# A graph network with feed-forward layers on one core: the norms, transposes and products of the two edge passes placed further apart, and the depth FFN on a line of its own

## The chip, the core and the metric

The program runs on one core of a Trainium2 chip. Five engines work side by side, each on its own queue in order: TensorE for matrix products (PE; its weight loads are listed as PEld), VectorE (DVE), ScalarE (ACT), GpSimd (POOL) and SyncE (SP, which here only issues DMAs). The measure is the device time of one execution in microseconds; a median of three runs stands for a kernel.

## The reference, cut to what matters

There are 12500 nodes of 256 numbers and 212500 edges, sorted by destination. Four layers follow each other, each on the layer norm of what came before, each added to it:

```python
edge_index = jnp.stack([src, dst])
x = x + _L0_gnn_ref(_layernorm(x), L0_gnn_weight, src, dst, edge_type_8, edge_weight)
x = x + _L0_ffn_ref(_layernorm(x)[None], ..., L0_ffn_wr, L0_ffn_br, L0_ffn_w1, L0_ffn_b1, L0_ffn_w2, L0_ffn_b2)[0]
x = x + _L1_gnn_ref(_layernorm(x), edge_index, L1_gnn_W, L1_gnn_att_src, L1_gnn_att_dst, L1_gnn_bias)
x = x + _L1_ffn_ref(_layernorm(x)[None], L1_ffn_Wg, L1_ffn_bg, L1_ffn_W1, L1_ffn_b1, L1_ffn_W2, L1_ffn_b2)[0]
```

- L0 gnn: for every edge the source row, multiplied by one of eight block-diagonal matrices and by the edge's weight, is summed at the destination.
- L0 ffn ("depths"): a score per node picks half of the nodes; for those `gelu(n @ w1 + b1) @ w2 + b2` with 1024 hidden units is weighted and added.
- L1 gnn: graph attention with 4 heads: softmax over the edges of a destination, weighted sum of the source rows, elu.
- L1 ffn: a gate of 8 experts; each node goes to its two best experts, 512 hidden units each.

## The kernel before, in words

**Stages.** First a table T0 of all eight products of every node is written to memory (97 stores of 1 MB). Then comes the first edge pass (`even_depths`), which also runs the depth FFN for every node; then the choice of the half (`choose`) and the combination; then the attention pass (`even_gat`), which also routes nodes to experts; last the experts (`slots`), 67 groups of 256 places.

**An edge pass.** Edges are taken in tiles of 128, 1661 of them. For each tile POOL gathers 128 rows from a table (L234), and PE multiplies them by a matrix S of 128 edges by 96 nodes (96 columns, each edge has a 1 or its weight at its destination; made by DVE for six tiles at once at L1012 and L1107). The products add up in PSUM in a bin of nodes (L1003): 512 nodes in the first pass, 256 in the second. A tile's window of 96 nodes sometimes lies across two bins; then each half has two products instead of one. In the trace every fp32 product of the program is two MATMUL and two LDWEIGHTS rows, so a tile has four rows, or eight across a bin's edge.

**Order.** The order on PE, DVE, ACT and SP is written out by hand. `Plan` is a list of (step, work); one step is one edge tile. At step t the gather of tile t is issued, at step t + 3 (first pass) its products follow. Gathers on POOL run free of this order: they wait only for a free buffer, of which the first pass has 16, one tile each; in the second pass a tile is fetched some 50 steps before it is used. A piece of work written as a generator goes on the plan too: `yield n` means that the rest comes n steps later. `Plan.queue(line, step, work)` runs the works of one line after each other. So when an engine's next instruction in this order has to wait, all that stands behind it on that engine waits too.

**When a bin of the first pass is full** (every 68 tiles), `summed` (L1046 to L1099) is queued on `line`: the node rows are loaded (SP), the sums copied out of PSUM (ACT L1052, DVE L1053), transposed back by PE (L195, `pt<-ident,aT`) and added to x (DVE L1060); the norm's statistics follow (DVE L214, L215, L201 to L208), then for each of up to four blocks of 128 nodes the normalized row `xn` (DVE L219), its transpose one step later (PE L195, `pt<-ident,xn`), the score (DVE L1073), x plus its norm (DVE L1075), and the copy into `xT` two steps later (L189 on ACT and L191 on DVE by turns). Then the FFN: for f of 8, two products with 512 columns (L1083) and the gelu (ACT L1085), one f every two steps; and for each block eight products with 256 columns (L1091) into a `pt` buffer, four to a step, then the bias (DVE L1097) and the store of Y (SP). The PSUM pools are `bin` (two buffers of two banks), `ph` (two) and `pt` (two).

**When 512 nodes of the attention pass are full**, `route` (L723 to L798) is queued on a line there. It computes the norm's statistics, and for each block `xn` (L219), one step later its transpose, one step later the copy to `xT`, one step later two products with 8 columns (L749) for the gate; then the choice on DVE, a count (L777, L778) and the scatter of the rows to their places (POOL).

Of the kernel before, what the change touches and what calls it, by code (L numbers as in the profile page):

```python
# [23 lines left out]
F32 = mybir.dt.float32  # L24
# [3 lines left out]
OP = mybir.AluOpType  # L28
# [7 lines left out]
P = 128  # L36
# [64 lines left out]
def gnn_ffn_kernel(ctx: ExitStack, tc: tile.TileContext, x, src, dst, etype, eweight, w_rel, wr, br,  # L101
                   fw1, fb1, fw2, fb2, W, att_src, att_dst, bias, Wg, bg, W1, b1, W2, b2, out):
    nc = tc.nc
    N, D = x.shape
# [88 lines left out]
    def transpose(o, i):  # L193
        k = i.shape[0]
        nc.tensor.transpose(o, i, ident[:k, :k])  # L195
# [22 lines left out]
    def normalized(o, xr, mv):  # L218
        nc.vector.tensor_scalar(o, xr, mv[:, 0:1], mv[:, 1:2], op0=OP.subtract, op1=OP.mult)  # L219
# [99 lines left out]
    with ExitStack() as pre:  # L319
# [63 lines left out]
        for i, (t, nat, around, dt) in enumerate(((NS, KSN, 0.0, F32), (NBR, NBN, -FAR, F32), (DM, DMN, 0.0, BF16))):  # L383
# [15 lines left out]
                                op=OP.subtract)  # L399
# [275 lines left out]
    def router(st):  # L675
# [50 lines left out]
        def route(ms, xg, wk, pst, psc, behind=None):  # L726


            G = len(ms)
            mv = wk.tile([P, 4, 2], F32, name="mv")  # L730
            ln_stats(xg[:, :, :D], mv[:, :G], wk)
            yield 3
            nc.vector.tensor_copy(xg[:, :G, D], node[:, ms[0]:ms[0] + G])
            nc.vector.tensor_copy(xg[:, :G, D + 1:], mv[:, :G, :])
            gt = wk.tile([P, 4, NE], F32, name="gt")
            pg = psc[0].tile([P, 4, NE], F32, name=psc[1])
            for i, m in enumerate(ms):
                xn = wk.tile([P, D], F32, name="xn")
                normalized(xn, xg[:, i, :D], mv[:, i, :])
                yield 1  # L740
                pt = pst[0].tile([P, 2, P], F32, name=pst[1])
                for k in range(2):
                    transpose(pt[:, k, :], xn[:, k * P:(k + 1) * P])
                yield 1
                xT = wk.tile([P, 2, P], F32, name="xT")
                evac(xT, pt)
                yield 1
                for k in range(2):
                    nc.tensor.matmul(pg[:, i, :], xT[:, k, :], Wgs[:, k, :], start=k == 0, stop=k == 1)  # L749
            yield 2  # L750
            nc.vector.tensor_tensor(gt[:, :G, :], pg[:, :G, :], bgB[:, None, :].to_broadcast([P, G, NE]), op=OP.add)

            mk = wk.tile([P, 4, NE], F32, name="mk")
            q1 = wk.tile([P, 4, NE, NE], F32, name="q1")
            q2 = wk.tile([P, 4, NE, NE], F32, name="q2")
            for i in range(G):
                mine = gt[:, i, :, None].to_broadcast([P, NE, NE])
                other = gt[:, i, None, :].to_broadcast([P, NE, NE])
                nc.vector.tensor_tensor(q1[:, i], other, mine, op=OP.is_equal)
                nc.vector.tensor_tensor(q2[:, i], other, mine, op=OP.is_gt)  # L760
            yield 1
            nc.vector.tensor_tensor(q1[:, :G], q1[:, :G], lower[:, :G], op=OP.mult)
            nc.vector.tensor_tensor(q2[:, :G], q2[:, :G], q1[:, :G], op=OP.add)
            nc.vector.tensor_reduce(mk[:, :G, :], q2[:, :G], axis=AX.X, op=OP.add)
            nc.vector.tensor_scalar(mk[:, :G, :], mk[:, :G, :], 1.5, None, op0=OP.is_lt)
            if rows(ms[-1]) < P:
                nc.vector.tensor_scalar(mk[:, G - 1, :], mk[:, G - 1, :], real, None, op0=OP.mult)
            yield 1
            pair = q1
            for i in range(G):  # L770
                nc.vector.tensor_tensor(pair[:, i], mk[:, i, :, None].to_broadcast([P, NE, NE]),
                                        mk[:, i, None, :].to_broadcast([P, NE, NE]), op=OP.mult)
            nc.vector.tensor_tensor(pair[:, :G], pair[:, :G], lower[:, :G], op=OP.mult)
            yield 1

            pp_ = psc[0].tile([P, 2, 4, NE, NE], F32, name=psc[1])
            nc.tensor.matmul(pp_[:, 0, :G], before, pair[:, :G], start=True, stop=True)  # L777
            nc.tensor.matmul(pp_[:, 1, :G], ones, pair[:, :G], start=True, stop=True)  # L778
            yield 2
            pos = q2  # L780
            for i in range(G):
                nc.vector.tensor_tensor(pos[:, i], pp_[:, 0, i], run, op=OP.add)
                nc.vector.tensor_tensor(run, pp_[:, 1, i], run, op=OP.add)
            yield 1
            nc.vector.tensor_tensor(pos[:, :G], pos[:, :G], turn[:, None].to_broadcast([P, G, NE, NE]), op=OP.mult)
            nc.vector.tensor_tensor(pos[:, :G], pos[:, :G], start[:, None].to_broadcast([P, G, NE, NE]), op=OP.add)
            nc.vector.tensor_tensor(pos[:, :G], pos[:, :G], pair[:, :G], op=OP.mult)
            to = wk.tile([P, 4], F32, name="to")
            nc.vector.tensor_reduce(to[:, :G], pos[:, :G].rearrange("p g e f -> p g (e f)"), axis=AX.X, op=OP.add)
            toI = wk.tile([P, 4], I32, name="toI")  # L790
            nc.vector.tensor_copy(toI[:, :G], to[:, :G])
            yield 3
            for i, m in enumerate(ms):
                n = rows(m)
                if i:
                    yield 2
                with tc.issue_after(behind().ins) if behind else nullcontext():
                    filled.append(to_slots(toI[:n, i:i + 1], xg[:n, i, :]))  # L798
# [227 lines left out]
    def even_depths(AD, lcC):  # L1026


        with ExitStack() as md:
# [8 lines left out]
            with ExitStack() as r1:  # L1038
# [2 lines left out]
                psA = r1.enter_context(tc.tile_pool(name="r1_pa", bufs=2, space=PSUM))  # L1041
                psh = r1.enter_context(tc.tile_pool(name="r1_ph", bufs=2, space=PSUM))
                pst = r1.enter_context(tc.tile_pool(name="r1_pt", bufs=2, space=PSUM))
                plan, line = Plan(), []

                def summed(b, sums):  # L1046
                    ms = [m for m in range(b * BIN // P, (b + 1) * BIN // P) if m < NM]
                    G = len(ms)
                    xg = wk.tile([P, 4, D], F32, name="xg")
# [1 line left out]
                    aT = wk.tile([P, 2, BIN], F32, name="aT")  # L1051
                    nc.scalar.activation(aT[:, 0, :G * P], sums[0][:, :G * P], AF.Copy)  # L1052
                    nc.vector.tensor_copy(aT[:, 1, :G * P], sums[1][:, :G * P])  # L1053
                    yield 3
                    for i, m in enumerate(ms):
                        pt = pst.tile([P, 2, P], F32, name="pt")
                        for k in range(2):
# [2 lines left out]
                        nc.vector.tensor_tensor(X[:, m, :], xg[:, i, :], pt.rearrange("p k j -> p (k j)"), op=OP.add)  # L1060
                    mv = wk.tile([P, 4, 2], F32, name="mv")
                    ln_stats(X[:, ms[0]:ms[0] + G, :], mv[:, :G], wk)
                    yield 1
                    xT = wk.tile([P, 2, 4 * P], F32, name="xT")
                    for i, m in enumerate(ms):
                        xn = wk.tile([P, D], F32, name="xn", bufs=2)
                        normalized(xn, X[:, m, :], mv[:, i, :])
                        yield 1
                        pt = pst.tile([P, 2, P], F32, name="pt")
                        for k in range(2):  # L1070
                            transpose(pt[:, k, :], xn[:, k * P:(k + 1) * P])
                        junk = wk.tile([P, D], F32, name="junk")
                        nc.vector.scalar_tensor_tensor(junk, xn, 1.0, wrB, op0=OP.mult, op1=OP.mult,  # L1073
                                                       accum_out=WT[:, m:m + 1])
                        nc.vector.tensor_tensor(X[:, m, :], X[:, m, :], xn, op=OP.add)  # L1075
                        yield 2
                        evac(xT[:, :, i * P:(i + 1) * P], pt)
                    yield 2
                    hT = wk.tile([P, KH, 4 * P], F32, name="hT")
                    for f in range(KH):  # L1080
                        ph = psh.tile([P, 4 * P], F32, name="ph")
                        for k in range(2):
                            nc.tensor.matmul(ph[:, :G * P], w1s[:, k, f * P:(f + 1) * P], xT[:, k, :G * P],  # L1083
                                             start=k == 0, stop=k == 1)
                        nc.scalar.activation(hT[:, f, :G * P], ph[:, :G * P], AF.Gelu_apprx_tanh, bias=b1s[:, f:f + 1])  # L1085
                        yield 2
                    yield 1
                    for i, m in enumerate(ms):
                        py = pst.tile([P, D], F32, name="pt")
                        for f in range(KH):  # L1090
                            nc.tensor.matmul(py, hT[:, f, i * P:(i + 1) * P], w2s[:, f, :],  # L1091
                                             start=f == 0, stop=f == KH - 1)
                            if f % 4 == 3:
                                yield 1
                        yield 1
                        y = wk.tile([P, D], F32, name="y", bufs=2)
                        nc.vector.tensor_tensor(y, py, b2B, op=OP.add)  # L1097
                        n = rows(m)
                        nc.sync.dma_start(Y[m * P:m * P + n, :], y[:n])  # L1099

# [705 lines left out]
```

## Time and profile before

| | us |
|---|---|
| median of 3 runs | 6287.21 (6270.61 to 6287.57) |
| the profiled execution's own time | 7111.5 |
| its span, first to last instruction | 7109.7 |
| first pass: first to last gather | 468.1 to 2909.2 |
| attention pass: first to last gather | 3178.8 to 5987.5 |
| last stage (experts): first to last product | 6128.6 to 7092.9 |
| mean granted TensorE clock | 0.733 |

The profiled execution is 824 us longer than the median, so a stage read from it is not a stage of the timed runs; what is worked out from it has to be carried over. The profile has, for each engine, the time in which it was busy; in its second part the span in 40 slices, with the clock that TensorE was granted in each; the chain of waits that ended last; and groups of instructions by line, with the mean of one. The trace behind it also gives these for any stretch of time, and the clock as a list of stretches at full and at half rate, each a whole number of 3.413 us long.

### The profile page before, as it was taken

How to read it: one execution, taken by the hardware profiler on the slowest of the kernel's cores; microseconds unless marked ns; L12 is line 12 of the kernel's file. 1: busy time of each engine (PE TensorE's matmuls, PEld its weight loads, DVE VectorE, ACT ScalarE, POOL GpSimd, SP SyncE). 2: the span in 40 equal slices, each digit the busy share in tenths (PEclk: the TensorE clock that was granted, in tenths of full speed). 3: DMA queues.
4: the chain of work that ended last, by engine and by line, in shares of the span. 5: the costliest groups of instructions: out<-in, count | busy, mean ns of one | idle time of the engine just before them, and what ended most of it. 6: DMA issues, size and time to landing. Idle time of an engine off the chain costs nothing.

```text
span 7109.7 us, 79724 instructions
## 1 busy us (share of the span) xinstructions
PE 5659.9 (80%) x28484; PEld 4914.0 (69%) x28484; DVE 3019.7 (42%) x7766; ACT 771.3 (11%) x1619; POOL 3699.1 (52%) x3731
## 2 busy tenths in 40 slices
PE   6977887787788877663777777878777778699999
PEld 3446666666677666553776777777777777688887
DVE  6642323223322333373555555556555555422221
ACT  2320000000000000040000000000000000122222
POOL 0026666666666666276656565666666564221111
PEclk9986877888778877785555555555565555799999
DMA  7763333333333333264444444444444443465553
GB/s 245 301 232 96 98 100 101 102 101 97 100 101 102 100 98 101 69 206 114 114 111 115 107 113 113 111 114 117 110 116 112 109 112 86 144 220 183 184 172 117
DMA packets 471792, 914.69 MB, mean 129 GB/s; under 512 B 83656, under 2 KB 307655, under 8 KB 458747
## 3 DMA queue, kind: packets, MB, share of 16 engines
q0 software_dynamic: 173280, 472.25, 23.9%
q1 hardware_dynamic: 298096, 437.15, 19.7%
q8 instruction: 230, 3.77, 0.2%
q14 instruction: 186, 1.52, 0.1%
HBM read 728.21 MB, written 185.63 MB: 129 GB/s over the span
## 4 chain that ended last, share of the span: by engine, by line
PE 55%; issue 17%; DVE 12%; another core or an unknown queue 9%; POOL 3%; DMA 2%; ACT 1%; SPq 0%; DVEq 0%; POOLq 0%; ACTq 0%
PE bin L1003 32%; PE pm L469 5%; PE ph L1083 5%; PE pt L1091 5%; PE pt L195 2%; DVE rows L1380 2%; POOL out_dram L946 1%; PE pt L749 1%; PE ph L932 1%; PE py L942 1%; DVE ln_st L214 1%; DVE S L1012 1%; PE px L1342 1%; PE py L1182 1%
## 5 line engine op out<-in xcount | busy, mean ns | idle before, releaser
L234 POOL DMA_INDIRECT rows<-T1A,srcC x1661 | 1644.0, 990 | 1053.1 <-issue 439.5
L234 POOL DMA_INDIRECT row<-T,rowC x1661 | 1649.4, 993 | 854.0 <-issue 306.0
L1003 PE MATMUL bin<-S,rows 128*128 128x96 f32 (+5 forms) x8756 | 1889.7, 388 | 244.8 <-issue 218.0
L1003 PEld LDWEIGHTS bin<-S,rows 128*128 128x128 f32 x8756 | 1814.5, 307 | 282.6 <-issue 252.9
L1003 PEld LDWEIGHTS bin<-S,row 128*128 128x128 f32 x7700 | 1247.4, 244 | 240.5 <-issue 219.5
L1003 PE MATMUL bin<-S,row 128*128 128x96 f32 (+5 forms) x7700 | 1263.2, 324 | 102.8 <-issue 99.6
L1012 DVE TENSOR_TENSOR S<-lcC,col 128x576 f32<-128x576 f32 x554 | 416.2, 751 | 501.6 <-PE bin L1003 212.2
L1380 DVE TENSOR_TENSOR rows<-rows,pw 128x1536 f32<-128x1536 f32 x277 | 483.2, 1745 | 120.0 <-remote 36.5
L195 PE MATMUL pt<-ident,xn 128*128 128x128 f32 x1052 | 225.7, 331 | 375.1 <-DVE xn L219 216.0
L1083 PE MATMUL ph<-xT,w1s 128*128 128x512 f32 (+1 forms) x800 | 419.0, 653 | 123.6 <-ACT hT L1085 79.1
L946 POOL DMA_INDIRECT out_dram<-y,toI x134 | 132.4, 988 | 698.2 <-DVE y L945 688.5
L932 PE MATMUL ph<-xT,we 128*128 128x256 f32 x2144 | 477.8, 381 | 2.0 <-DVE xT L191 2.0
L942 PE MATMUL py<-w,hT 128*128 128x256 f32 x2144 | 473.5, 379 | 0.0
L195 PEld LDWEIGHTS pt<-ident,xn 128*128 128x128 f32 x1052 | 155.9, 179 | 430.4 <-issue 290.2
L942 PEld LDWEIGHTS py<-w,hT 128*128 128x128 f32 x2144 | 407.4, 190 | 55.4
L932 PEld LDWEIGHTS ph<-xT,we 128*128 128x128 f32 x2144 | 405.0, 191 | 55.7 <-DVE xT L191 2.6
L1091 PE MATMUL pt<-w2s,hT 128*128 128x256 f32 x1568 | 379.0, 385 | 4.3 <-issue 4.1
L469 PE MATMUL pm<-BD,xT 128*128 128x512 f32 x784 | 352.5, 603 | 12.8 <-ACT xT L189 12.3
L945 DVE TENSOR_TENSOR y<-py,xs 128x256 f32<-128x256 f32 x134 | 56.8, 424 | 645.0 <-PE py L942 625.4
L1083 PEld LDWEIGHTS ph<-xT,w1s 128*128 128x128 f32 x800 | 151.2, 209 | 240.1 <-issue 155.3
L189 ACT ACTIVATE xT<-pt 128x256 f32<-128x256 f32 x214 | 82.3, 384 | 2124.0 <-PE pt L195 744.8
L1091 PEld LDWEIGHTS pt<-w2s,hT 128*128 128x128 f32 x1568 | 284.7, 191 | 37.4 <-issue 6.1
(307 smaller groups left out, 4618.0 us busy)
## 6 DMA issues: line engine op xcount, KB each, us to landing
T<-tb SPq DMA_DIRECT2D x97, 1024.0 KB
we<-in_L_ffn_W_dram SPq DMA_DIRECT2D x134, 512.0 KB
w<-in_L_ffn_W_dram SPq DMA_DIRECT2D x134, 512.0 KB
dmB<-DMN SPq DMA_DIRECT2D x277, 192.0 KB
row<-T,rowC POOLq DMA_INDIRECT x1661
rows<-T1A,srcC POOLq DMA_INDIRECT x1661
xg<-in_x_dram SPq DMA_DIRECT2D x48, 512.0 KB
xs<-XS SPq DMA_DIRECT2D x67, 259.0 KB
```

The lines of the kernel that those rows point to most:

```text
L189: nc.scalar.activation(dst_ap, src_ap, AF.Copy)
L195: nc.tensor.transpose(o, i, ident[:k, :k])
L234: return nc.gpsimd.indirect_dma_start(out=o, out_offset=None, in_=table, in_offset=bass.IndirectOffsetOnAxis(ap=idx, axis=0))
L469: nc.tensor.matmul(pm, xT[:, k, :], BD[:, k, r4:r4 + 4, :], start=True, stop=True)
L932: nc.tensor.matmul(ph[:, f - f2, :], we[j][:, k, f * P:(f + 1) * P], xT[:, k, :], start=k == 0, stop=k == 1)
L942: nc.tensor.matmul(py, hT[:, j, f, i * P:(i + 1) * P], w2[j][:, f, :], start=j == 0 and f == 0, stop=j == 1 and f == KE - 1)
L946: ins = nc.gpsimd.indirect_dma_start(out=out, out_offset=bass.IndirectOffsetOnAxis(ap=toI[:, i:i + 1], axis=0), in_=y, in_offset=None, bou ...
L1003: nc.tensor.matmul(open_[b][k][:, lo - b * size:hi - b * size], lhs(k), S[:, lo - base:hi - base], start=False, stop=last[b] == t and (siz ...
L1012: nc.vector.tensor_tensor(S[:, :n], lcC[:, t:t + n, None].to_broadcast([P, n, WIN]), col[:, None, :WIN].to_broadcast([P, n, WIN]), op=OP.i ...
L1083: nc.tensor.matmul(ph[:, :G * P], w1s[:, k, f * P:(f + 1) * P], xT[:, k, :G * P], start=k == 0, stop=k == 1)
L1091: nc.tensor.matmul(py, hT[:, f, i * P:(i + 1) * P], w2s[:, f, :], start=f == 0, stop=f == KH - 1)
L1380: nc.vector.tensor_tensor(r, r, group[g]["w"][:, o:o + c, :, None].to_broadcast([P, c, H, CH]), op=OP.mult)
```

## The change

Four things move. (1) In `route`, the four normalized blocks are made first, one per step; three steps later the transposes follow, two steps apart, each with its copy two steps behind; five steps later the gate products, one block per step. (2) In `summed` the same: four more steps before the first transpose, a step more before the norms, all four `xn` first (four buffers instead of two), then a pause of eight steps, then the transposes, each with its copy three steps behind. (3) The FFN becomes a generator of its own, `fed`, on a second line, `later`, which starts eight steps after the copies. Its first products come one matmul per step or two, the gelu two steps behind them, then a pause of six steps, then the second products, two every two steps: 62 steps in all. (4) The second products go into a `ph` buffer instead of a `pt` one.

```diff
             gt = wk.tile([P, 4, NE], F32, name="gt")
+            xns, xTs = [], []
+            for i, m in enumerate(ms):
+                xns.append(wk.tile([P, D], F32, name="xn", bufs=4))
+                normalized(xns[i], xg[:, i, :D], mv[:, i, :])
+                yield 1
+            yield 3
+            for i, m in enumerate(ms):
+                pt = pst[0].tile([P, 2, P], F32, name=pst[1])
+                for k in range(2):
+                    transpose(pt[:, k, :], xns[i][:, k * P:(k + 1) * P])
+                yield 2
+                xTs.append(wk.tile([P, 2, P], F32, name="xT", bufs=4))
+                evac(xTs[i], pt)
+            yield 5
             pg = psc[0].tile([P, 4, NE], F32, name=psc[1])
             for i, m in enumerate(ms):
-                xn = wk.tile([P, D], F32, name="xn")
-                normalized(xn, xg[:, i, :D], mv[:, i, :])
+                for k in range(2):
+                    nc.tensor.matmul(pg[:, i, :], xTs[i][:, k, :], Wgs[:, k, :], start=k == 0, stop=k == 1)
                 yield 1
...
-            yield 2
+            yield 1
...
-                plan, line = Plan(), []
+                plan, line, later = Plan(), [], []
...
-                    yield 3
+                    yield 7
                     for i, m in enumerate(ms):
                         pt = pst.tile([P, 2, P], F32, name="pt")
...
-                    yield 1
+                    yield 2
                     xT = wk.tile([P, 2, 4 * P], F32, name="xT")
+                    xns = []
                     for i, m in enumerate(ms):
-                        xn = wk.tile([P, D], F32, name="xn", bufs=2)
+                        xn = wk.tile([P, D], F32, name="xn", bufs=4)
                         normalized(xn, X[:, m, :], mv[:, i, :])
-                        yield 1
-                        pt = pst.tile([P, 2, P], F32, name="pt")
-                        for k in range(2):
-                            transpose(pt[:, k, :], xn[:, k * P:(k + 1) * P])
+                        xns.append(xn)
                         junk = wk.tile([P, D], F32, name="junk")
...
+                        yield 1
                         nc.vector.tensor_tensor(X[:, m, :], X[:, m, :], xn, op=OP.add)
-                        yield 2
+                        yield 1
+                    yield 8
+                    for i, m in enumerate(ms):
+                        pt = pst.tile([P, 2, P], F32, name="pt")
+                        for k in range(2):
+                            transpose(pt[:, k, :], xns[i][:, k * P:(k + 1) * P])
+                        yield 3
                         evac(xT[:, :, i * P:(i + 1) * P], pt)
-                    yield 2
+                    plan.queue(later, plan.now + 8, fed(ms, xT))
+
+                def fed(ms, xT):
+
+                    G = len(ms)
                     hT = wk.tile([P, KH, 4 * P], F32, name="hT")
                     for f in range(KH):
                         ph = psh.tile([P, 4 * P], F32, name="ph")
                         for k in range(2):
                             nc.tensor.matmul(ph[:, :G * P], w1s[:, k, f * P:(f + 1) * P], xT[:, k, :G * P],
                                              start=k == 0, stop=k == 1)
+                            yield 2 if k else 1
                         nc.scalar.activation(hT[:, f, :G * P], ph[:, :G * P], AF.Gelu_apprx_tanh, bias=b1s[:, f:f + 1])
-                        yield 2
-                    yield 1
+                    yield 6
                     for i, m in enumerate(ms):
-                        py = pst.tile([P, D], F32, name="pt")
+                        py = psh.tile([P, 4 * P], F32, name="ph")
                         for f in range(KH):
-                            nc.tensor.matmul(py, hT[:, f, i * P:(i + 1) * P], w2s[:, f, :],
+                            nc.tensor.matmul(py[:, :D], hT[:, f, i * P:(i + 1) * P], w2s[:, f, :],
                                              start=f == 0, stop=f == KH - 1)
-                            if f % 4 == 3:
-                                yield 1
-                        yield 1
+                            if f % 2:
+                                yield 2
                         y = wk.tile([P, D], F32, name="y", bufs=2)
-                        nc.vector.tensor_tensor(y, py, b2B, op=OP.add)
+                        nc.vector.tensor_tensor(y, py[:, :D], b2B, op=OP.add)
```

## The prediction

> **What bounds the kernel now.** I read the page's clock row and chain first, then the busy times by stage.
>
> ```profile
> PEclk9986877888778877785555555555565555799999
> PE 55%; issue 17%; DVE 12%; another core or an unknown queue 9%; POOL 3%; DMA 2%; ACT 1%; SPq 0%; DVEq 0%; POOLq 0%; ACTq 0%
> ```
> ```profile
> 900.00:1400.00 500.00, 404.79 (x2174) 342.06 (x2174) 147.14 (x342) 34.33 (x55) 339.23 (x342) 0.80 0.35 101
> 4000.00:4800.00 800.00, 618.36 (x3337) 591.95 (x3337) 447.97 (x1054) 32.80 (x70) 495.66 (x502) 0.57 0.43 113
> 6200.00:7110.00 910.00, 889.91 (x4234) 782.86 (x4232) 217.06 (x727) 231.35 (x556) 155.66 (x158) 0.99 0.55 177
> ```
> (Columns: span, busy PE, weight loads, DVE, ACT, POOL, then clock.) The change touches the first two stretches. In the last PE is 98% busy at full clock. The two passes run PE at 0.80 and 0.57 of its clock. Both take more than PE's busy time, so PE also waits. For the first pass, 900 to 2900 us, the groups by shape and the waits:
>
> ```profile
> L234 POOL DMA_INDIRECT row<-T,rowC x1361 | 1351.6, 993 | 649.5 <-issue 246.9 <-PE bin L1003 221.0 <-remote 104.3
> L1083 PE MATMUL ph<-xT,w1s 128*128 128x512 f32 x640 | 345.0, 666 | 113.0 <-ACT hT L1085 74.6 <-issue 26.0 <-DVE xT L191 12.4
> ```
> ```profile
> POOL row L234 <- PE bin L1003: 221.0, 348, 2.8
> PE pt L195 <- DVE xn L219: 108.3, 24, 10.2
> PE ph L1083 <- ACT hT L1085: 74.6, 19, 6.3
> PE pt L195 <- DVE mv L208: 60.6, 10, 7.6
> ```
> A gather takes 0.993 us and the median gap after it, 0.305 us, waits for nothing: 1.298 us a tile. The pass takes 2441 us over 1661 tiles, 1.470 us. The difference is POOL waiting for buffers that PE frees late, and PE is late because it stands at a transpose until DVE has made `xn`, or at a product until the gelu has freed PSUM.
>
> **The clock.** Two neighbouring stretches, both with PE busy throughout:
>
> ```profile
> 1286.00:1290.00 4.00, 4.00 (x38) 4.00 (x38) 0.01 (x1) 0.00 (x0) 2.72 (x3) 1.00 0.84 230
> 1290.00:1294.00 4.00, 4.00 (x22) 4.00 (x21) 0.00 (x0) 0.00 (x0) 2.81 (x3) 0.52 0.32 92
> ```
> PE did 38 products, then 22. Rows of the same form are 213 ns apart in the cold state and 112 ns in the warm one (edge products); the FFN's are 853 and 429 ns (512 columns), 427 and 216 ns (256). I counted the moving columns in each 3.413 us window of the clock: the 150 cold windows before a rise have 1509 to 2048 (5th to 95th percentile), the 150 warm ones before a fall at most 1497 (95th), the warm ones that stay warm at least 2226 (5th). The cold windows that stay cold have at most 1536 (95th). So some 1500 to 1536 columns a window decide. An edge tile has 384 whatever its split.
>
> The Trainium skill ("TensorE: Matmul & The Clock Gate", part 1) says that activity in a window of 3413 ns opens the clock and an idle window closes it. The window length agrees; "busy" doesn't, for a busy PE fell to half rate here. By the page's rule, fewer idle gaps would warm the attention pass too, and its products would halve: PE would fall under the gather rate, and up to 2809 - 1759 x 1.289 = 542 us of the profile could go. By the rows, a tile there has 384 columns and about 80 of other work, at 1.6 us 990 a window: it stays cold. I take the rows.
>
> **First pass, part by part.** Nothing is added or removed; all products, DVE and ACT operations stay, and so do the one x load and the four Y stores per bin on SP. The load stands ten steps ahead of its first reader instead of six, so a Y store ahead of it on SP, now later by a bin's length, may be some us late at no cost. The `fed` line has 62 steps in 68: it fits, and `xT`, with one buffer, is read 24 steps before it is written again. *(a)* The waits for `xn` and `mv` (108.3 + 60.6) and for `xT` (12.4) go: eight steps, 10 us, stand between, longer than all but the worst wait (10.2). DVE isn't stretched: 147 of 500 us. *(b)* Of ph's 74.6 us behind the gelu all goes, three steps instead of two. Together 256 of 2000 us, 312 over the pass, if nothing else binds. *(c)* The FFN's 32768 columns per bin were in a burst; now they lie over 62 steps: 384 + 528 = 912 a step, at 1.3 us 2390 a window, so warm nearly throughout. PE's work per bin is then 315 edge rows x 0.112 + 32 x 0.429 + 64 x 0.216 + 32 transposes x 0.109 = 66 us, against 68 x 1.298 = 88 of gathering. POOL binds: 1661 x 1.298 = 2156, a gain of 285 in the profile.
>
> *(d)* The tail after the last gather (69 us before) has the next to last bin's FFN and the last bin's chain beside it: 0 taken, +-15.
>
> **Attention pass**, 3400 to 6000 us:
>
> ```profile
> PE pt L749 <- ACT xT L189: 77.0, 12, 14.8
> PE pt L195 <- DVE xn L219: 51.1, 9, 16.9
> ```
> Removable: 128 of 2600, 138 over the pass. But a part is no real wait:
>
> ```profile
> 3895.27 0.69 PE L195 MATMUL pt<-ident,xn 128*128 128x128 f32 x2 [1.18 <-DVE xg L733]
> 3912.11 0.38 ACT L189 ACTIVATE xT<-pt 128x256 f32<-128x256 f32 x1 [35.23 <-remote]
> ```
> The copy to `xT` waits only for PE's semaphore, and that comes 16 us after the transposes, with PE idle meanwhile: a completion reported late. I take 100 in the profile. `route` ends 11 steps later, in a line of 68: free; so is the later scatter, except at the very end (a few us). Profile: 7110 - 285 - 100 = 6725.
>
> **From the profile to the median.** The median is 824 us lower. The table and the experts are spaced at PE's own row times, so the difference must lie in the passes: their 2441 + 2809 = 5250 us are some 4427 in a timed run. The late completions explain much of it: 10.1% of the first pass's chain and 13.0% of the attention pass's are "another core or an unknown queue", some 630 us. What is left there to remove is what DVE or ACT really makes late: in the first pass 108.3 + 60.6 + 12.4 and half of ph's 74.6, 219 of 2000, 267 over the pass; in the attention pass 51.1 and half of 77.0, 97 over the pass: 364. But gathering takes 2156 + 1759 x 1.289 = 2267, together 4423, just the 4427, if its spacing in timed runs is that of the trace: then nearly nothing can be gained. If the 0.305 us gap is the profiler's, all 364 and more can. I can't see this from one profile. Between 0 and 364 I take 155, nearer the traced spacing: 6287 - 155 = 6130.
>
> **Rivals.**
>
> *The gathers already bind.* For it: the sum 4423 above. Against: a kernel with these PE stalls can't run exactly at the gather rate in both passes, and the attention pass on a cold PE needs 5.3 rows x 0.213 + 0.3 = 1.4 us a tile, more than POOL. Gain 10 to 70, some 6245; at its lower end no change.
>
> *Untraced gathers are faster.* At about 1.0 us a tile PE was the bound throughout; warm it needs 66 us a bin, POOL 68. The first pass goes from some 2150 to 1750 us, the attention pass gains little: 5880.
>
> *Slower: the first pass locks cold.* Place: `fed`. Today's FFN burst has up to 3840 columns a window and re-warms PE by itself; evenly spread work can't. On a cold PE a step takes 4.64 x 0.213 + 0.80 (FFN) + 0.10 (transposes) = 1.89 us for 926 columns, 1670 a window, only 9% over 1536. It decides at 2.06 us a step: 0.17 us of waiting per tile is enough, or bin edges, where a tile has eight rows and a cold window 1200 columns. Locked, a bin takes 128 us instead of some 88; if that holds for a sixth of the bins or a run of steps around each edge, it is 160 us, near 6450. For it: the pauses of six steps with edge products alone, 1000 columns a window, cool PE twice a bin. Against: outside edges the sum is above the threshold, and 16 buffered rows let PE catch up.
>
> **How the numbers follow.** Likeliest, 0.42: part of the stalls is worth time, 6130 (its own range 6030 to 6230). Gathers bind already: 0.20, of it 0.12 faster and 0.08 no change. Faster gathers: 0.20. Slower: 0.18. That no change happens at all is excluded: the new order on PE has an FFN product after nearly every edge tile. A measurement of this kernel tells a change from none at about 0.3%, 19 us. So faster 0.74, same 0.08, slower 0.18. The range runs from 5850, leaving out the lower half of the fast case (0.1), to 6320, leaving out the worse half of the slow one (0.1).
>
> **What would show it.** In the changed profile the first pass has gathers at most 1.33 us apart (first to last some 2160 us), a clock of 0.9 or more from 900 to 2700 us, no wait of `pt` for `xn` or `mv` above 20 us in all, and POOL's waits for `bin` near 0. The attention pass keeps its clock of 0.57 and loses the two waits. Wrong would be: a clock under 0.7 in the first pass (locked cold); gathers no closer although the waits are gone (another bound); a profile 400 us shorter with an unchanged median (the profiler's lag was what the change removed).

## The result, and the profile after

The changed kernel takes 6338.36 us (median of 4 runs, 6331.24 to 6341.71) beside 6283.52 us (6270.61 to 6287.57) of the kernel before in the same session: a ratio of 1.0086 with a 95% interval of 1.0074 to 1.0098. It is slower by 0.9%, 55 us. Forecast were 6130 us.

The profiled execution of the changed kernel took 6331.24 us, its span is 6329.5 us. So it stands for the timed runs. The page of before did not: its execution took 7111.5 us, as long as all 19 executions of the kernel before in one session below (7089 to 7120 us), while its own timed runs took 6270.61 to 6287.57.

The clock row and the chain on the page of the changed kernel:

```profile
PEclk9995889888988888877555655555555656999999
PE 56%; issue 14%; DMA 12%; DVE 10%; POOL 6%; ACT 0%; SPq 0%; POOLq 0%; DVEq 0%; ACTq 0%
```
The part "another core or an unknown queue", 9% before, is gone from the chain. Busy times of three stretches, one in each stage (columns as in the prediction):

```profile
900.00:1400.00 500.00, 436.81 (x2320) 345.94 (x2320) 155.76 (x355) 37.68 (x60) 376.85 (x377) 0.87 0.39 111
3600.00:4400.00 800.00, 720.92 (x4118) 702.66 (x4117) 554.10 (x1311) 41.48 (x88) 612.25 (x617) 0.59 0.53 139
5420.00:6260.00 840.00, 838.04 (x3989) 737.46 (x3989) 209.44 (x706) 220.52 (x530) 145.80 (x148) 1.00 0.59 189
```
The first pass runs at 0.87 of the clock instead of 0.80, the attention pass at 0.59. POOL gathers 377 tiles in the first of these stretches, 500 us, where the page of before had 342. The largest waits of POOL and of PE in the first pass, 700 to 2600 us:

```profile
POOL row L234 <- PE bin L1008: 225.7, 623, 2.5
PE bin L1008 <- DMA row<-T,rowC: 208.8, 301, 4.0
```
(Line 1008 is line 1003 of the kernel before.) PE's waits for `xn`, `mv` and `xT` are all gone, and what PE waits for now is the gathered rows. Nor does it wait for a `ph` buffer, which the second products now share with the first: beside the rows, only 0.2 us of waiting are left from 900 to 2600 us. Yet from the first gather to the last the pass takes 2210.1 us, 1.331 us a tile. The forecast had 2156 us. And POOL's longest wait for PE is 2.5 us, where the pause that belongs to a gather is 0.305 us.

### The profile page after: what moved, and what is told of

It reads as the page before. It is cut to its first block, busy times and chain, and to the rows that moved or that the text cites. A ratio compares the mean times of both kernels' runs of the same rounds, so it can differ in the third digit from the quotient of the medians.

```text
span 6329.5 us, 79655 instructions
## 1 busy us (share of the span) xinstructions
PE 5556.3 (88%) x28484; PEld 4749.1 (75%) x28484; DVE 3018.5 (48%) x7766; ACT 771.1 (12%) x1619; POOL 3729.3 (59%) x3731
## 4 chain that ended last, share of the span: by engine, by line
PE 56%; issue 14%; DMA 12%; DVE 10%; POOL 6%; ACT 0%; SPq 0%; POOLq 0%; DVEq 0%; ACTq 0%
PE bin L1008 32%; DMA row<-T,rowC 10%; PE ph L1098 7%; PE pm L469 6%; PE ph L1106 3%; POOL rows L234 3%; DVE rows L1394 2%; PE pt L195 2%; POOL out_dram L951 2%; PE ph L937 2%; PE py L947 2%; DMA rows<-T1A,srcC 1%; PE pt L753 1%; PE px L1356 1%; POOL row L234 1%
## 5 line engine op out<-in xcount | busy, mean ns | idle before, releaser
L1008 PE MATMUL bin<-S,rows 128*128 128x96 f32 (+5 forms) x8756 | 1813.6, 383 | 44.1 <-DVE rows L1394 43.6
L1008 PEld LDWEIGHTS bin<-S,rows 128*128 128x128 f32 x8756 | 1744.1, 301 | 70.4 <-DVE rows L1394 48.6
L1008 PEld LDWEIGHTS bin<-S,row 128*128 128x128 f32 x7700 | 1219.5, 228 | 606.5 <-DMA row<-T,rowC 316.4
L1008 PE MATMUL bin<-S,row 128*128 128x96 f32 (+5 forms) x7700 | 1283.0, 312 | 241.6 <-DMA row<-T,rowC 234.9
L1098 PE MATMUL ph<-xT,w1s 128*128 128x512 f32 (+1 forms) x800 | 503.8, 722 | 0.0
L1106 PE MATMUL ph<-w2s,hT 128*128 128x256 f32 x1568 | 419.1, 394 | 0.0
L1106 PEld LDWEIGHTS ph<-w2s,hT 128*128 128x128 f32 x1568 | 277.9, 196 | 23.6
L469 PEld LDWEIGHTS pm<-BD,xT 128*128 128x128 f32 x784 | 145.5, 191 | 189.4 <-issue 154.1
L195 PE MATMUL pt<-ident,xn 128*128 128x128 f32 x1052 | 202.6, 307 | 83.2 <-DVE xn L219 37.1
L1101 ACT ACTIVATE hT<-ph,b1s 128x512 f32<-128x512 f32 (+1 forms) x200 | 135.8, 679 | 1069.5 <-PE ph L1098 1069.5
```

The lines of the kernel that those rows point to most:

```text
L469: nc.tensor.matmul(pm, xT[:, k, :], BD[:, k, r4:r4 + 4, :], start=True, stop=True)
L1008: nc.tensor.matmul(open_[b][k][:, lo - b * size:hi - b * size], lhs(k), S[:, lo - base:hi - base], start=False, stop=last[b] == t and (siz ...
L1106: nc.tensor.matmul(py[:, :D], hT[:, f, i * P:(i + 1) * P], w2s[:, f, :], start=f == 0, stop=f == KH - 1)
```

## The experiments

### The kernel before once more, unchanged

The comparison needed an execution of the usual length. The kernel was not edited.

> The kernel before, unchanged, to have an ordinary execution of it in a trace (the one shown took 7111 us, the median 6284). Theory G (the gathers bind both passes in a timed run): first to last gather of the first pass 2170 to 2200 us, of the attention pass 2250 to 2290 us, the waits of the transposes for xn still there but covered by buffered rows. Theory P (PE's stalls bound the kernel before and the change lost elsewhere): first pass above 2260 us, with gathers that wait for PE.

Measured: 6272.84 us. Its first pass takes 2162.4 us, 1.303 us a tile, its attention pass 2277.7 us. Two stretches of this execution, then POOL's waits from 700 to 2600 us and PE's from 900 to 2600 us:

```profile
900.00:1400.00 500.00, 477.63 (x2458) 400.46 (x2457) 173.04 (x407) 35.67 (x58) 382.46 (x386) 0.78 0.39 114
3600.00:4400.00 800.00, 714.56 (x4106) 693.77 (x4107) 552.67 (x1294) 41.05 (x87) 612.01 (x618) 0.59 0.52 138
```
```profile
POOL row L234 <- PE bin L1003: 182.8, 600, 0.3
POOL row L234 <- issue: 171.8, 564, 0.3
```
```profile
PE bin L1003 <- DMA row<-T,rowC: 73.6, 150, 1.8
```
This is the profile that the prediction needed. POOL never waits longer than 0.3 us: it gathers one tile after the other, 382.46 us busy and 386 pauses of 0.305 us, which is all of the 500 us. In the attention pass POOL has 98 scatters beside 1661 gathers; from the first gather of that pass to the last its pauses beyond 0.305 us add up to 1.1 us. (Over 3200 to 5200 us it is busy 1513.13 us in 1527 instructions, and with their pauses that is 1979 of 2000 us; the last gather is at 5171.3 us.) The stalls of the page (108.3 us behind `xn`, 60.6 behind `mv`, 74.6 behind the gelu) are not there: all that PE waits for in these 1700 us is rows. Both passes already ran at the rate of POOL, so a change that leaves the gathers as they are could not make them faster. It remains to find what became slower.

### The two parts of the change alone

The first kernel has the new order in `route` and the old `summed`, the second the new `summed` and `fed` and the old `route`.

```diff
 e_route: before, with
+            xns, xTs = [], []
+            for i, m in enumerate(ms):
+                xns.append(wk.tile([P, D], F32, name="xn", bufs=4))
...
 e_depths: before, with
+                    plan.queue(later, plan.now + 8, fed(ms, xT))
...
```

> The route part of the change alone. If this part is the loss: about +0.9% (6340 us). If the depth part is the loss: within 0.2% of before, for the gathers bind the attention pass and its stalls are covered. If route's stalls really cost time: 30 to 90 us faster.

> The depth part of the change alone (norm distances, the FFN on its own line, its PSUM pool). If it is the loss: +0.9% (6340 us), with the first pass some 50 us longer than in the trace of before. If route is the loss: within 0.2% of before.

Measured: `route` alone 6278.87 us, ratio 0.9999 (0.9991 to 1.0007); the depth part alone 6335.02 us, ratio 1.0084 (1.007 to 1.0098). The whole loss is in the depth part. The first pass is 2166.3 us with the one and 2211.3 us with the other. In `route` a wait that is there in the usual execution did go: PE's for `xn` between 2900 and 5150 us, in the kernel before

```profile
PE pt L195 <- DVE xn L219: 78.2, 21, 11.8
```
and none with the part alone. It was worth nothing, and POOL, whose pauses beyond 0.305 us are 1.1 us in this pass with the part and without it, sets the pace.

### Where the first pass loses it

POOL's pauses beyond 0.305 us add up to 43.4 us in the changed kernel's first pass, to 0 in the kernel before. All of them lie at 11 of the 24 bin edges (about every second one), 14 to 20 tiles after the edge's last tile, and there are 16 row buffers. One of these places, POOL's timeline of the changed kernel (start, duration, in brackets the time before it and what ended it):

```profile
1934.81 0.94 POOL L234 DMA_INDIRECT row<-T,rowC  x1 [0.30 <-PE bin L1008]
1936.22 0.94 POOL L234 DMA_INDIRECT row<-T,rowC  x1 [0.47 <-PE bin L1008]
1939.63 1.04 POOL L234 DMA_INDIRECT row<-T,rowC  x1 [2.47 <-PE bin L1008]
1942.22 0.94 POOL L234 DMA_INDIRECT row<-T,rowC  x1 [1.54 <-PE bin L1008]
```
How late PE is can be taken from the end of a tile's gather to the end of its last product. Ahead of such an edge that is 2.6 to 3.6 us, and from the edge on it grows to 21.8 to 23.8 us. The 16 buffers last for 19.8 us of it (16 x 1.303, less the gather's own 1.0). At the other edges it reaches 5.7 to 7.8 us, at the first of all 9.6 us. What PE does at the edge of 1907 us, by stretches:

```profile
1893.00:1897.00 4.00, 1.07 (x8) 0.67 (x7) 2.38 (x4) 0.00 (x0) 3.08 (x4) 0.91 0.81 247
1897.00:1901.00 4.00, 3.68 (x17) 3.68 (x18) 0.00 (x0) 0.00 (x0) 3.09 (x4) 0.50 0.40 118
...
1910.00:1944.00 34.00, 34.00 (x108) 25.05 (x108) 3.63 (x5) 3.35 (x5) 23.12 (x25) 0.50 0.32 92
1944.00:1948.00 4.00, 4.00 (x22) 2.74 (x21) 0.00 (x0) 0.69 (x1) 2.66 (x4) 0.99 0.28 90
```
At 1893 us PE has little to do and loses its clock: the FFN pauses, and PE waits 2.86 us for the row of the next tile. In the same stretch the DMA engines are busy 0.81 of the time, where they have some 0.4 before and after; the load of the node rows was issued at 1892.51 us. That it delayed the row was not tested. From 1910 to 1944 us it is busy all of the time, 34.00 of 34.00 us, and has half of the clock all of the time. The timeline shows what with:

```profile
1910.08 2.05 PE L1098 MATMUL ph<-xT,w1s 128*128 128x512 f32 x2
1911.93 1.73 PE L1008 MATMUL bin<-S,row 128*128 128x80 f32 x8
1913.49 2.06 PE L1098 MATMUL ph<-xT,w1s 128*128 128x512 f32 x2
```
An edge tile has eight rows of 0.213 us, the product of the FFN two rows of 0.853 us: 3.41 us for 384 + 1024 = 1408 columns. That is one window of the clock, 3.413 us, and 1408 columns are fewer than 95% of the cold windows before a rise had in the trace of before (1509 and more). I counted the columns in each window from 1906 to 1940 us: nine of ten hold 1408, the tenth 768. The window at 1940.7 us, still cold, has 1792 columns, and from 1944.1 us on PE has full clock.

Why every second edge? `Plan.queue` starts a work in the step asked for if its line is empty, but one step after the one before it if that is still under way. `fed` is put on `later` some steps before the previous one ends, or after: in the first case it follows at once, in the second eight steps later, and the two cases take turns. In the trace the time from the last second product to the next first one is 16.6 to 19.6 us at one bin and 2.9 to 4.4 us at the next. In the long case the FFN begins 1.0 to 1.8 us after the product that clears the new bin, at the start of the edge, in the short one 6.4 to 9.0 us ahead of it.

So there are three theories. *Locked cold:* the long pause cools PE, and the FFN's first product meets tiles with eight rows, with which it can't get warm again. *Too much work at one place:* products of the FFN beside eight edge rows make PE late whatever its clock. *Another cause of the loss*, of which the POOL waits are only a part.

### The FFN's start moved

Two kernels put the FFN on its line with a delay of one step, and of twenty, instead of eight. The work and the steps inside `fed` stay the same.

```diff
-                    plan.queue(later, plan.now + 8, fed(ms, xT))
+                    plan.queue(later, plan.now + 1, fed(ms, xT))    (r1_start1)
+                    plan.queue(later, plan.now + 20, fed(ms, xT))   (r5_start20)
```

> The changed kernel with the depth FFN's line starting 1 step instead of 8 after the copies, so that its pause of 6 steps ends some 17 steps ahead of the bin's edge and not right at it. Theory L (PE goes cold in that pause, then meets eight edge rows a tile and the FFN's first products, stays cold there with 1408 columns a window, falls 22 us behind and uses up the 16 row buffers): the cold edges and POOL's waits go, first to last gather 2165 us instead of 2210, about 6285 us. Theory S (the even spread itself costs, wherever it lies): 6335 us still.

> The same start 20 steps after the copies: the FFN's first products begin only behind the bin's edge, the edge has edge products alone or the end of the FFN before. Theory L: PE may be cold at the edge, but without the FFN a cold tile of eight rows takes 1.7 us, so over ten tiles the lag grows by 4 us, not 17: no waits of POOL, 6285 us. Theory S: 6335 us.

Measured: with one step 6287.90 us, ratio 0.9992 (0.9984 to 1.0), the loss is gone; with twenty 6303.21 us, ratio 1.0026 (1.0015 to 1.0036), two thirds of it are. The pauses of POOL beyond 0.305 us are 1.8 and 11.8 us, the first pass 2170.3 and 2181.4 us.

With one step the start no longer takes turns: at every bin there is a pause of 9.2 to 11.8 us, and the FFN begins 7.8 to 9.5 us ahead of the product that clears the new bin. PE goes cold in the pause here too (window at 1873.8 us), but the first product of the FFN then stands beside a tile of four rows: 4 x 0.213 + 2 x 0.853 = 2.56 us for 1408 columns, 1877 a window. The next window, at 1877.2 us, has 1792 columns, and from 1880.7 us on PE is warm, before the edge. One edge is an exception:

```profile
1614.00:1618.00 4.00, 3.83 (x18) 2.18 (x16) 1.35 (x2) 0.69 (x1) 3.09 (x4) 1.00 0.33 94
1622.00:1650.00 28.00, 28.00 (x96) 21.76 (x96) 3.44 (x5) 2.96 (x5) 20.56 (x22) 0.50 0.36 103
```
PE comes to it warm, waits 0.99 us for a row at its start and loses its clock there. It is then busy throughout at half rate, 20.7 us late, and all of POOL's 1.8 us are at this edge.

With twenty steps I had expected 6285 us and missed by 0.3%. The start takes turns over four bins there: after the first bins, 20.7, 9.9 and some 3 us after the new bin is cleared and 5.2 to 7.3 us ahead of it. Where the FFN begins 20.7 us after, PE has 0.50 to 0.54 of the clock in the edge, but without the FFN it falls only 9.2 to 10.5 us behind, and POOL doesn't pause. Of the 11.8 us of pauses, 10.0 are at two edges where the FFN begins 7.3 and 5.6 us *ahead*:

```profile
917.00:942.00 25.00, 25.00 (x83) 18.80 (x82) 1.52 (x2) 2.06 (x3) 17.19 (x19) 0.50 0.33 96
1279.00:1304.00 25.00, 25.00 (x84) 19.18 (x84) 0.00 (x0) 2.06 (x3) 18.83 (x21) 0.50 0.37 106
```
At the three later edges with such a start PE has full clock and is at most 7.1 us late. So neither a cold PE at the edge nor an FFN begun early decides alone: what costs time is a cold PE that has edge rows and the FFN together.

### Fewer row buffers

If the loss is POOL waiting for the 16 buffers of rows while PE is late, fewer buffers make it dearer with the change and cost nothing without it.

```diff
-                rw = r1.enter_context(tc.tile_pool(name="r1_r", bufs=16))
+                rw = r1.enter_context(tc.tile_pool(name="r1_r", bufs=12))
```

> The changed kernel with 12 row buffers instead of 16. Theory L: a cold edge leaves PE 22 us behind, and 12 buffers cover 15.6 us instead of 20.8, so each of the 12 locked edges costs 5.2 us more: 6335 + 62, some 6400 us. Theory S: little change, under 10 us.

> The kernel before with 12 row buffers instead of 16. Its PE is never more than about 10 us behind the gathers, which 12 buffers (15.6 us) cover: theory L and theory S both expect no change, 6281 us. A loss here would say that fewer buffers cost by themselves.

Measured: the change with 12 buffers 6400.25 us, ratio 1.0178 (1.0163 to 1.0194), as expected; POOL's pauses are 113.6 us and the first pass 2278.4 us. The kernel before with 12 buffers 6295.1 us, ratio 1.0008 (1.0001 to 1.0015); the only pause of its pass is 4.5 us at its start. Lateness that uses up the buffers is there with the change alone (the kernel before is at most 11.7 us late at an edge), and each buffer covers 1.3 us of it. More than 16 buffers were not tried.

### Idle work added in the pause

These runs still move the FFN or the buffers. The last question is whether the clock itself is the cause. So PE got more to do, in the long pause alone; the FFN starts where it does in the changed kernel.

```diff
+                    if not later:
+                        plan.follow(plan.now, filled())
                     plan.queue(later, plan.now + 8, fed(ms, xT))
 
+                def filled():
+                    for n in (1, 2, 1, 2, 1, 1):
+                        pf = psh.tile([P, 4 * P], F32, name="ph")
+                        nc.tensor.matmul(pf, w1s[:, 0, :P], w1s[:, 1, :4 * P], start=True, stop=True)
+                        yield n
```

> The changed kernel with idle work added: where no depth FFN is under way when the next one is put on its line, six products of 512 columns (two weights with each other, their result is never read) are spread over the eight steps ahead of it. That is 72 products, 144 rows of 0.429 us, 62 us more work for TensorE in the first pass, and the FFN still starts in the step in which it starts in the changed kernel, 2 us after the new bin is opened, in twelve of the bins. Theory (TensorE has gone to half rate in the 14 steps without FFN ahead of such a bin edge, and that is what makes it 22 us late): the added columns bring it back to full rate before the edge, POOL waits no more than some 5 us for rows over the pass instead of 43, first pass about 2170 us, time about 6290 (the ratio to before 0.999 to 1.002), so with more work it is faster by some 45 us than the changed kernel. Rival (FFN products beside the eight edge rows of a tile are too much for TensorE at this place, whatever its clock): the lateness at these edges stays at 22 us or grows by the added work, up to 6 times 1.7 us at each of twelve edges, and the time is 6335 to 6400.

Measured: 7092.16 us beside 7104.93 us of the kernel before, ratio 0.9983 (0.9969 to 0.9998). That decides nothing, for here both kernels took some 800 us more than in the other experiments. It does show that the change with the added work has no large gain there either: the first pass takes 2542.8 us (2441.1 on the page of before), the attention pass 2703.2 us (2808.7). It was run again, with the changed kernel beside it:

> The kernel with the six added products again, since all executions of the last run, those of the kernel before among them (7104.93 us), were of the long kind of the page (7111.5 us), in which other waits decide. If the kernel before takes some 6285 us here: theory 6290 us (ratio 0.999 to 1.002, first pass about 2170 us, POOL's waits for rows at most some 5 us), rival 6335 to 6400. If it takes some 7105 again: about 7092, the ratio 0.9983 of the last run.

> The changed kernel, unaltered, beside the same runs of the kernel before. If that takes some 6285 us: 6338 (ratio 1.0085), first pass 2210 us with 43 us of POOL's waits. If it takes some 7105 (the long executions of the page): theory, the stalls that the page shows are due to TensorE's late completions, and the change takes some of them away, so a ratio of 0.97 to 0.998, at most the 385 us that the prediction took from this profile; rival, they only move to other instructions, a ratio of 1.00 to 1.02.

Measured: with the added work 6286.91 us, ratio 1.0012 (1.0003 to 1.002); the changed kernel 6337.58 us, ratio 1.009 (1.0075 to 1.0105), both against 6277.85 us. With the added work the edge shown above comes 18.3 us earlier, at 1888.9 us. The pause ahead of it and the 34 us in it, and POOL's longest wait from 700 to 2600 us:

```profile
1874.70:1878.70 4.00, 1.61 (x8) 1.61 (x8) 0.91 (x2) 0.00 (x0) 3.08 (x4) 0.60 0.64 216
1878.70:1882.70 4.00, 4.00 (x10) 2.32 (x10) 0.00 (x0) 0.00 (x0) 3.09 (x4) 0.54 0.37 107
1887.70:1891.70 4.00, 4.00 (x23) 2.54 (x22) 0.00 (x0) 0.00 (x0) 3.08 (x4) 1.00 0.42 115
1891.70:1925.70 34.00, 32.16 (x198) 24.40 (x198) 11.03 (x27) 6.10 (x9) 25.78 (x28) 1.00 0.36 103
```
```profile
POOL row L234 <- PE bin L1008: 189.2, 621, 0.3
```
PE has 72 products more, 144 rows, and the kernel is 51 us faster than without them. PE still goes cold in the pause, but the added products make it warm again before the edge, and the FFN meets a warm PE in the same step. In these 34 us PE does 198 rows in 32.16 us, where cold it did 108 in 34.00. Every edge but the first is warm, PE is at most 9.7 us late at any, and POOL doesn't pause once beyond its 0.3 us. The clock is the cause; "too much work at one place" falls, and so does "another cause": the first pass went from 2213.5 to 2170.6 us, 43 of the 51 us, and 7 more lie between the passes.

Two executions of the changed kernel say the same without an edit. At the edge near 1005 us the FFN begins after the long pause in both. In the first, one cold window before it happens to have 1536 columns and the clock opens; in the second (`r8_after`) the three cold windows before it have at most 1440 and it stays shut. The changed kernel first as profiled with the result, then as `r8_after`:

```profile
1005.00:1031.00 26.00, 26.00 (x157) 19.45 (x156) 5.39 (x8) 5.41 (x8) 19.91 (x20) 1.00 0.35 101
1006.00:1032.00 26.00, 26.00 (x86) 19.69 (x86) 0.00 (x0) 2.06 (x3) 19.60 (x22) 0.50 0.37 105
```
Warm, PE is at most 6.0 us late there and POOL doesn't pause; cold, PE is 22.5 us late and POOL pauses 5.4 us.

## Why the prediction was wrong

Taken between the two profiles of usual length, the first pass has lost 47.7 us (2162.4 to 2210.1), of which 43.4 are POOL's pauses and 4 gathers that are 2.4 ns longer each. The attention pass lost 6.2 us, the time between the passes 3.7, what follows the last gather 1.8. That is 59 us of spans that differ by 58.5. The 6.2 us are gathers and scatters 3.5 ns longer each; their mean differs by up to 7 ns between executions, also with `route` alone, whose time is that of the kernel before, so they are not laid to the change.

- **What bounds the kernel now: wrong, and it carried the rest.** The prediction read PE stalls as the cause of 1.470 us a tile, and priced them. A tile takes 1.303 us in the usual execution, and that is the gather (0.998) and its pause (0.305): PE's stalls cost nothing there.
- **From the profile to the median: the step that failed first.** It found that the gathers' 4423 us are just the 4427 us of the timed passes, and said that then nearly nothing can be gained. It still took 155 us, between 0 and 364. The sum was right: there was nothing to gain. The argument set against it, that a kernel with these stalls can't run at the gather rate, rests on stalls that the timed runs don't have. The rival "the gathers already bind" had the bound right (its 10 to 70 us of gain were 0), and "untraced gathers are faster" is excluded: the traced execution of 6272.84 us, with gathers 1.303 us apart, is as fast as the timed runs.
- **(a), (b), the waits that go.** They go, as the order says: PE's waits for `xn`, `mv`, `xT` and the gelu are 0 after. In the first pass they were nothing in a usual execution to begin with; in the attention pass, where 100 us were taken in the profile for `xn` and `xT`, 78.2 us for `xn` were real and still worth nothing, since POOL was the bound. *(d)*, the tail behind the last gather of the first pass, taken at 0 +-15, grew by 3.7 us (63.1 to 66.8).
- **(c), "warm nearly throughout": the second step that failed, and the one that made the kernel slower.** Over the pass the clock did rise, from 0.78 to 0.87 (900 to 1400 us), but at 11 of 24 edges PE stayed at half rate. The step averaged the FFN over 62 steps of 68 and laid two pauses of six steps between. It did not work out where `Plan.queue` puts the second pause: at every other bin 14 steps from product to product, and its end at the start of the edge. That the busy time of PE fell, 1810 to 1688 of 1900 us, was worth nothing to a pass that waits for POOL.
- **The rival "the first pass locks cold".** Its place (bin edges) and its start (PE cools in the pause) are what happened, and 16 buffers did not let PE catch up. It had a chance of 0.18 and stood against the forecast. Its size, 160 us, was about three times too large: only every second edge locks, and only what is left of 22 us of lateness after 16 buffers is paid, 43.4 us at 11 edges, 3.9 us each. "A cold window 1200 columns" at an edge was 1408.
- **The rule weighed against the rows.** Here too the rows were right: a PE that was busy in every window from 1910 to 1940 us kept half of its clock. The attention pass, too, stayed at 0.59 without its waits for `xn`; that is the weaker sign, for they were 78.2 of some 2250 us.

## What to carry to other kernels

Before a stall is priced, compare the profiled execution with the timed runs. Here it was 13% longer, and the waits priced in its first pass were not there in an execution of the usual length; what held was the sum of the gathers' own durations and pauses, which fitted the timed passes. An even spread of PE's work is not safe in itself: for each pause, work out the columns per clock window of what follows on a cold PE, at its densest place (rows x their cold duration against the window), and see to it that PE is warm when it gets there. An early start of the heavy products does that in most bins here, not in all. To see whether a cold clock is the cause, add work to the pause: if the kernel gets faster, it is.

## What the runs showed of the hardware

- PE can be busy without a gap for 34 us and stay at half rate: nine of ten windows held 1408 moving columns. A row of an edge product takes 0.112 us warm and 0.213 us cold in the changed kernel's first pass, whether it has 16 columns or 96, so splitting a tile in two doubles PE's time and leaves its columns as they were. 72 products whose result nobody reads made the kernel 51 us faster.
- The same kernel can take 13% longer elsewhere: in one session, on one chip, 19 executions of the kernel before took 7089 to 7120 us, on the three chips of the other experiments 6269 to 6302 us. Whether the chip or the session made the difference was not tested. In the long ones PE waits for "issue" inside the edge products (in the first run with added work 178.4 us in 276 waits from 900 to 2900 us, where the usual execution of the kernel before shows none), and in the trace of before a completion reached ACT 16 us late (the prediction's lines of 3895 and 3912 us). What causes this stays open; whether the unaltered change gains or loses there was not seen.
